# Stores on another queue, a residual chunk per group, inverse steps half a group later

## The chip, the cores and the metric

The kernel runs on one core of one Trainium2 chip. The metric is the device time of one execution in microseconds (us), as the median of repeated runs. Engines are named as in the profile: PE (TensorE), DVE (VectorE), ACT (ScalarE), POOL (GpSimd), SP (SyncE, which here only issues DMAs).

## The reference

Two layers work on x (2 batches, 128 channels, 64 x 64 positions = 4096 tokens). Layer 0 is a block of neighbourhood attention and an MLP. Layer 1 is what the change touches the end of:

```python
t = to_tokens(x)
t = t + attention(layernorm(t))          # 4096 x 4096 scores, per batch
t = t + ffn(layernorm(t))                # spectral filters over the sequence
# ffn, for the chosen branch (of 4): u of shape (b, sl, d)
U_plus  = irfft(rfft(phi)[:, :, None] * rfft(u)[:, None])      # 16 filters, length 8192
U_minus = the same of u with alternating signs, signs put back
out = einsum('btkd,k,kde->bte', U_plus, sigma**0.25, M_plus) + the same with U_minus, M_minus
out = out + sum over 3 lags of shifted u @ M_u[lag]
```

## The kernel before, in words

**Stages.** Layer 0 and the attention of both batches fill the first part (to about 1155 us of the span). A transition (about 1155 to 1197 us) finishes the last token chunks. Then comes the mixing stage, 40 groups of matmuls in about 725 us, and a tail of some 32 us that writes the output.

**The end of the attention.** `after(b, c)` (L1119) is a generator that takes one chunk of 512 tokens from attention to the transform: the softmax quotient and the residual (DVE), a copy into the layout of the scratch tensor `rd` and its store (L1141, L1142), the layernorm (its power is taken by POOL, L174), the transpose (L202), and matmuls with the transform `tr` (L1191, L1205). `store` (L1158) brings the products to DRAM as `us`: ACT copies them from PSUM (L1171), sums and differences are taken (L1176, one half by POOL, one by DVE at the end), and DMAs go out. A chunk has two full stores, of two DMAs of 256 KB each, and a small one, of eight DMAs of 32 KB each (destination 2 x 32 rows of 512 bytes, L1183). `fresh` (L1108) decides who issues: as long as `crowd_[0]` is a list, the DMAs are queued for POOL; once it is None, in the transition, they go out at once on SP (L1110), and the staging tiles `wide` are then cut from the attention's large buffers `e` and `et` (L1163, L1165), two of each. Three small stores (24 DMAs) and five full ones fall into this part. Between these steps PE computes the short lags (L1228), which DVE and ACT bring from PSUM into `xa` (L1249, L1245); PE's and SP's orders are those of the program text, and PE has five PSUM banks for all of these.

**The mixing stage.** A group takes four bins of one batch; a batch has 20 groups (`GROUPS`). For every group:

- four bursts (`burst`, L1588, PE L1597, 16 matmuls each) make the group's y from a block `ct` and an input `ut`, both loaded by SP (four DMAs at L1490, one at L1498). DVE and ACT copy a burst's four PSUM slots (`pc`, four in all) into y (L1602), two each. There are two y tiles, and the bursts of the following group run inside the present one, at k = 0 and 8 of l = 0 and 1.
- 32 projections (`project`, L1612, PE L1616, four matmuls each) add up in four PSUM tiles `acc`, for l in 0..1 and k in 0..15. A burst and eight projections make a quarter of a group.
- `mixed_bins` (L1622) copies `acc` out as `af` (L1626, two by DVE, two by ACT), and POOL folds `af` into the store of bins `ob` in ten operations (L1627 to L1645).

The y tiles of the stage's start lie where the `wide` tiles were: as built, the first copy of y waits for the last small store to have landed.

**The inverse.** When 64 bins of a batch are complete, a generator `back` (L1647) is appended to `rest`, and after a batch's last group `finished` (L1708). A step is taken at k = 4 of each l (L1774): it multiplies what the step before had transposed (L1654; DVE adds the products to `xa`, L1660), and transposes the next two places of `ob` (L1667, ACT copies them, L1668). The first step of `back` only transposes, the last only multiplies. `finished` begins in the same way (L1682) and goes on with products (L1697). A `back` falls behind the 16th group of each batch, `finished` behind the 20th of the first.

**The residual.** `residuals` (L1728) reads `rd` back in 16 chunks: four SP loads (L1734) into one tile `rt`, a 32 x 32 transpose in place by DVE (L1740), an addition to `xa` by POOL (L1742). It is advanced once a burst (L1772); a chunk takes five advances: one for each load, one for the transpose and the addition. DVE's and POOL's orders are made by a scheduler at build time; PE's and SP's are those of the text.

Of the kernel before, what the change touches and what calls it, by code (L numbers as in the profile page):

```python
# [14 lines left out]
P = 128  # L15
# [82 lines left out]
BC = 64  # L98
# [4 lines left out]
def kernel(  # L103
# [16 lines left out]
    nc = tc.nc  # L120
# [14 lines left out]
    for c in range(4):  # L135
# [23 lines left out]
        out=flip, in_=flip, compare_op=ALU.not_equal, fill=1.0, base=1 - QT * QT, pattern=[[0, 2], [1, QT * QT]],  # L159
# [80 lines left out]
    with l0a:  # L240
# [34 lines left out]
        def table(ci, h, eng):  # L275
# [16 lines left out]
            out=gavg, in_=gavg, compare_op=ALU.is_ge, fill=0.0, base=0,  # L292
# [3 lines left out]
            out=gavg, in_=gavg, compare_op=ALU.is_ge, fill=0.0, base=3,  # L296
# [581 lines left out]
    with ap_:  # L878
# [6 lines left out]
        def bank():  # L885
# [6 lines left out]
            out=tr.rearrange("p h e c -> p (h e) c"),  # L892
            in_=nc.inline_tensor(t_in, "t_in").ap().rearrange("(h p) c -> p h c", p=P),
# [208 lines left out]
        def room():  # L1102

            while len({n for _, n, *_ in queued_}) > 3:
                send_one()
            turns_[1] += 1

        def fresh(to, part, by=nc.gpsimd):  # L1108
            if crowd_[0] is None:
                nc.sync.dma_start(out=to, in_=part)  # L1110
                return
            queued_.append((turns_[0], turns_[1], by, to, part))

# [5 lines left out]
        def after(b, c):  # L1119
# [11 lines left out]
            rest = sp.tile([P, 4], F32, tag="rest", name="rest")  # L1131
# [22 lines left out]
            to = zc[b][:, par, s0 : s0 + 2 * P * FB].rearrange("p (c e f) -> p e f c", e=2, f=FB)  # L1154
# [3 lines left out]
            def store(pu, n, r0, m, ri):  # L1158

                if crowd_[0] is None:  # L1160
                    free_[0] = not free_[0]
                    if free_[0]:
                        wide_ = ep.tile([P, 2048], F32, tag="e", name="wide").rearrange("p (a c) -> p a c", c=512)  # L1163
                    else:
                        wide_ = ep.tile([P, 4, 512], F32, tag="et", name="wide", bufs=2)  # L1165
                for s in range(2):
                    if crowd_[0] is None:
                        both, ub = wide_[:, s], wide_[:, 2 + s].rearrange("p (i c) -> p i c", i=2)
                    else:
                        both = sp.tile([P, 512], F32, tag="uo", name="uo", bufs=2)  # L1170
                    nc.scalar.copy(both[:, 0 : 2 * n], pu[s][:, 0 : 2 * n])  # L1171
                    if crowd_[0] is not None:
                        room()
                        ub = sp.tile([P, 2, 256], F32, tag="ub", name="ub", bufs=4)
                    for sgn, op in enumerate((ALU.add, ALU.subtract)):
                        adder[sgn].tensor_tensor(ub[:, sgn, 0:n], both[:, 0:n], both[:, n : 2 * n], op)  # L1176
                    to = us[b, par, r0 : r0 + m, :, :, 2 * hh + s, 2 * fp : 2 * fp + 2]
                    if ri is not None:
                        fresh(to[:, :, ri].rearrange("k g f d -> k g (f d)"), ub)
                        continue  # L1180
                    for sgn in range(2):
                        for f in range(2):
                            fresh(to[:, sgn, :, f].rearrange("k i d -> i k d"), ub[64 * f : 64 * f + 64, sgn, 0:P])  # L1183

            for r0, c0 in row_tiles:
                for ri in range(2):
# [272 lines left out]
        for hh in range(SG // 2):  # L1459
            for e in range(2):  # L1460
# [3 lines left out]
                    out=pns[hh, e].rearrange("p k l f -> p (k l) f"),  # L1464
                    in_=bass.AP(
                        phi_pad.tensor, P - FB + (2 * P * hh + e) * FB, [[2 * FB, P], [PHW, 2 * KF], [1, LG]]
                    ),
# [100 lines left out]
    with ExitStack() as cv:  # L1568
# [8 lines left out]
        def sums(j):  # L1577
            return ps_p.tile([P, 512], F32, tag=f"acc{j}", name="acc")
# [6 lines left out]
        KG = 4  # L1585
        GROUPS = K2 // KG

        def burst(y, kl):  # L1588

            ct, ut = ahead.pop(0)  # L1590
            pcs = [slot() for _ in range(4)]
            for par in range(2):
                cv_ = ct[:, :, 0 : 2 * (FB + 1 + par) * KF].rearrange("p o (l c) -> p o l c", l=2)[:, :, :, 0:TK]
                at = slice(1, 3) if par else slice(0, 4, 3)
                for j in range(4):
                    rows_ = slice(32 * j, 32 * j + 32)
                    nc.tensor.matmul(  # L1597
                        pcs[j].rearrange("p (g o c) -> p o g c", g=4, o=2)[:, :, at], lhsT=ut[rows_, par, :],
                        rhs=cv_[rows_], start=True, stop=True,
                    )  # L1600
            for j in range(4):
                (nc.scalar.copy if j % 2 else nc.vector.tensor_copy)(  # L1602
                    y[:, :, :, 4 * kl + j, :], pcs[j].rearrange("p (g x k) -> p k g x", g=4, k=KF)
                )
            if to_load:
                b_, q_ = to_load.pop(0)
                ahead.append((blocks(q_), inputs(b_, q_)))

        def new_y():
            return cp.tile([P, KF, 4, 4 * KG, 2 * FB], F32, tag="y", name="y", bufs=2)  # L1610

        def project(y, acc, l, k):  # L1612

            for j in range(4):
                rows_ = slice(32 * j, 32 * j + 32)
                nc.tensor.matmul(  # L1616
                    acc[j][:, 0:256], lhsT=(mmi if l else mpl)[rows_, k, :],
                    rhs=y[rows_, k, 2 * l : 2 * l + 2].rearrange("p s n x -> p (s n x)"),
                    start=(l == 0 and k == 0), stop=(l == 1 and k == KF - 1),
                )  # L1620
# [107 lines left out]
        def residuals():  # L1728

            for b in range(NB):  # L1730
                for c in range(NT // 4):
                    rt = cp.tile([P, 4, 4, 32], F32, tag="rt", name="rt", bufs=1)
                    for q in range(4):
                        nc.sync.dma_start(  # L1734
                            out=rt[32 * q : 32 * q + 32].rearrange("p h j i -> p h (j i)"),
                            in_=rd[b, c].rearrange("(h p) q r -> q p h r", h=4)[q],
                        )
                        yield
                    flat = rt.rearrange("p h j i -> p (h j i)")
                    nc.vector.transpose(flat, flat)  # L1740
                    xs = xa[b][:, c * 512 : (c + 1) * 512].rearrange("p (j h r) -> p h j r", j=4, h=4)
                    nc.gpsimd.tensor_tensor(xs, rt, xs, ALU.add)  # L1742
                    yield

        to_add = residuals()
        order_ = [(b, q) for b in range(NB) for q in range(K2)]
        to_load = order_[len(first_blocks) :]
        ahead = list(first_blocks)
        rest = []
        with tc.manual_schedule(engines={mybir.EngineType.PE, mybir.EngineType.SP}):  # L1750
            y = new_y()
            for i in range(4):
                next(lags, None)
                burst(y, i)
            for _ in lags:
                pass
            lags_.close()


            obp = cv.enter_context(tc.tile_pool(name="ob", bufs=1))  # L1760
            ob = obp.tile([P, NB, K2 // BC, 4, 2, BC, 2 * FB], F32, name="ob")
            ob_last = obp.tile([P, NB, 2, 4, LAST, 2 * FB], F32, name="ob_last")
            groups = [(b, g) for b in range(NB) for g in range(GROUPS)]
            for i, (b, g) in enumerate(groups):
                final = i + 1 == len(groups)
                following = None if final else new_y()
                acc = [sums(j) for j in range(4)]
                for l in range(2):
                    for k in range(KF):
                        if following is not None and k % 8 == 0:  # L1770
                            burst(following, 2 * l + k // 8)
                            next(to_add, None)  # L1772
                        project(y, acc, l, k)
                        if rest and k == 4:  # L1774
                            if next(rest[0], None) is None:
                                rest.pop(0)
                mixed_bins(b, g, acc, nc.vector if final else nc.gpsimd)
                y = following
                if (g + 1) * KG % BC == 0:
                    rest.append(back(b, g * KG // BC, [(par, f) for par in range(2) for f in range(FB)]))  # L1780
                if g + 1 == GROUPS and not final:
                    rest.append(finished(b))
            for steps in rest:
                for _ in steps:
                    pass
# [21 lines left out]
        for h in range(2):  # L1807
            o = cp.tile([P, HQ, 2, 2, FB, 2], F32, tag="o", name="o", bufs=2)
            for par in range(2):
                for a in range(4):  # L1810
                    to = place_of(o, par, a)
# [100 lines left out]
```

## Time and profile before

| what | value |
|---|---|
| median of 3 runs | 1960.01 us (1958.05 to 1962.58) |
| the profiled execution: its own time | 1956.34 us |
| its span, first to last instruction | 1954.4 us |
| busy in the span: PE, DVE, ACT, POOL | 1885.4, 960.3, 734.7, 775.9 us |
| PE busy, 1155 to 1197 us (42 us) | 31.63 us, granted clock 0.88 |
| PE busy, 1197 to 1922 us (725 us) | 718.39 us, granted clock 1.00 |
| L1740 DVE transpose of `rt` | 16 times, 711 ns each |
| L1742 POOL addition of `rt` | 16 times, 1271 ns each |

Times in the text are places in the span, in us from its start. A row of the timeline gives the start, the length, the engine, the line, the operation with output and inputs, how many were merged (x) and, in brackets, the idle time of the engine before it and what ended that. Merged matmuls overlap, so the distance between the starts of two bursts tells more than busy time: it is the time of a quarter of a group. "Granted clock" is the share of full speed that PE was given.

### The profile page before, as it was taken

Reading aid. Unit: us, or ns where it says so; the run is one execution under the profiler, and the core shown is the slowest. Engines: PE = TensorE matmul, PEld = TensorE weight load, DVE = VectorE, ACT = ScalarE, POOL = GpSimd, SP = SyncE. Lnnn points to the kernel's source line nnn. Section 1 sums busy time; section 2 is a strip of 40 time slices with the busy share of each in tenths; the row PEclk is TensorE's granted clock in tenths of the full one; section 3 lists DMA queues with packets and bytes.
Section 4 is the critical chain, followed back from the end, with each engine's and each line's share of the span. In section 5 each row is a group of like instructions: output and inputs, shape, how many; then the busy total and the mean of one; then the engine's idle time right before and its main releaser. Section 6 shows DMA issues by size and latency. Waiting matters only on the chain. (4 is left out here: it accounts for less than half of the span.)

```text
span 1954.4 us, 50851 instructions
## 1 busy us (share of the span) xinstructions
PE 1885.4 (96%) x20376; PEld 1343.4 (69%) x20376; DVE 960.3 (49%) x3002; ACT 734.7 (38%) x1742; POOL 775.9 (40%) x1255
## 2 busy tenths in 40 slices
PE   6899998999999999999999998999999999999997
PEld 4677776444444444444444446999998999999986
DVE  5799997454554534454534463333333333333332
ACT  2789887323233323232332242222222222222221
POOL 4366886423743337633443341223332221222211
PEclk8999999999999999999999999999999999999999
DMA  4222221666876545987876422333232223222211
GB/s 155 63 60 59 63 61 41 146 188 215 228 212 190 166 126 164 262 231 227 240 206 180 118 90 74 79 78 79 77 80 60 69 70 90 69 68 67 66 40 45
DMA packets 260394, 234.55 MB, mean 120 GB/s; under 512 B 128095, under 2 KB 214127, under 8 KB 252736
## 3 DMA queue, kind: packets, MB, share of 16 engines
q1 hardware_dynamic: 232290, 133.87, 28.2%
q10 hardware_dynamic: 8126, 58.04, 7.7%
q0 software_dynamic: 19744, 39.39, 6.7%
q8 instruction: 162, 2.65, 0.6%
q14 instruction: 72, 0.59, 0.1%
HBM read 135.59 MB, written 95.45 MB: 118 GB/s over the span
## 5 line engine op out<-in xcount | busy, mean ns | idle before, releaser
L1602 DVE COPY y<-pc 128x512 f32<-128x512 f32 x320 | 205.8, 685 | 326.4 <-PE pc L1597 317.2
L1616 PE MATMUL acc<-y,mpl 32*128 32x256 f32 x5120 | 322.8, 379 | 1.8 <-DVE af L1626 1.7
L1602 ACT COPY y<-pc 128x512 f32<-128x512 f32 x320 | 171.9, 589 | 397.9 <-PE pc L1597 385.0
L1616 PE MATMUL acc<-y,mmi 32*128 32x256 f32 x5120 | 313.7, 375 | 0.0
L1616 PEld LDWEIGHTS acc<-y,mpl 32*128 32x128 f32 x5120 | 291.0, 186 | 10.5 <-DVE af L1626 4.3
L1616 PEld LDWEIGHTS acc<-y,mmi 32*128 32x128 f32 x5120 | 291.2, 185 | 2.8
L1058 PE MATMUL other<-e,tok 128*128 128x512 f32 x448 | 227.3, 593 | 0.0
L932 ACT ACTIVATE e<-bank 128x512 f32<-128x512 f32 x216 | 129.0, 598 | 257.8 <-PE bank L927 253.6
L927 PE MATMUL bank<-cm 128*128 128x512 f32 x432 | 221.8, 600 | 0.0
L1627 POOL TENSOR_TENSOR af<-af 128x512 f32<-128x512 f32 x39 | 49.7, 1275 | 428.4 <-DVE af L1626 415.4
L1597 PE MATMUL pc<-ct,ut 32*128 32x256 f32 x2560 | 210.3, 377 | 6.7 <-ACT y L1602 5.9
L985 PE MATMUL own<-et,tok 128*128 128x512 f32 x448 | 210.3, 593 | 5.0 <-DVE et L975 5.0
L1597 PEld LDWEIGHTS pc<-ct,ut 32*128 32x128 f32 x2560 | 173.3, 186 | 12.0 <-ACT y L1602 6.8
L975 DVE STREAM_TRANSPOSE et<-et 128x512 f32<-128x512 f32 x216 | 134.3, 679 | 87.9 <-DMA et<-eb 87.9
L985 PEld LDWEIGHTS own<-et,tok 128*128 128x128 f32 x448 | 84.6, 190 | 112.7 <-issue 94.2
L1176 POOL TENSOR_TENSOR ub<-uo 128x256 f32<-128x256 f32 (+1 forms) x160 | 99.8, 662 | 148.9 <-ACT uo L1171 136.0
L1058 PEld LDWEIGHTS other<-e,tok 128*128 128x128 f32 x448 | 81.6, 191 | 88.7 <-issue 82.4
L927 PEld LDWEIGHTS bank<-cm 128*128 128x128 f32 x432 | 76.3, 190 | 76.1 <-issue 70.8
L546 ACT ACTIVATE p<-p,mn 128x196 f32<-128x196 f32 x256 | 114.4, 449 | 14.4 <-DVE mn L536 13.8
L1094 POOL DMA_DIRECT2D us<-ub x158 | 107.6, 710 | 9.4 <-DMA us<-ub 7.3
L943 ACT ACTIVATE e<-bank 128x512 f32<-128x512 f32 (+1 forms) x72 | 32.5, 455 | 124.6 <-DVE bank L941 113.3
L536 DVE CUSTOM_DVE_ANT_0 p<-bank,tab 128x196 f32<-128x196 f32 x256 | 76.4, 353 | 4.9 <-PE bank L523 4.7
(274 smaller groups left out, 2639.6 us busy)
## 6 DMA issues: line engine op xcount, KB each, us to landing
eb<-e ACTq DMA_DIRECT2D x54, 1024.0 KB
et<-eb SPq DMA_DIRECT2D x216, 256.0 KB
ut<-us SPq DMA_DIRECT2D x156, 128.0 KB
us<-ub POOLq DMA_DIRECT2D x54, 256.0 KB, 3.6
vw<-vd SPq DMA_DIRECT2D x256, 49.0 KB
ct<-gs SPq DMA_DIRECT2D x312, 40.0 KB
ct<-gs SPq DMA_DIRECT2D x312, 32.0 KB
vd<-v SPq DMA_DIRECT2D x128, 32.0 KB
```

The costliest lines, as they stand in the source:

```text
L536: nc.vector.tensor_tensor_reduce(t[name + "p"][:, h, :], t[name + "S"][h][:, 0:KEYS], tab[:, ci, h, :], 1.0, 3.0e38, ALU.add, ALU.min, t[n ...
L546: nc.scalar.activation(p, p, AF.Exp, bias=t[name + "mn"][:, h : h + 1], scale=-1.0, accum_out=t["den"][:, u, h : h + 1],)
L927: nc.tensor.matmul(ps.rearrange("p (q t j) -> p q t j", q=4, t=4), lhsT=cm[b][:, n * P : (n + 1) * P], rhs=keys.rearrange("p (t q j) -> p ...
L932: nc.scalar.activation(e, ps.rearrange("p (q t j) -> p q t j", q=4, t=4), AF.Exp, bias=0.0, scale=ASCALE)
L975: in_place(nc.vector.transpose(part, part))
L985: nc.tensor.matmul(out_, lhsT=tok[b][:, n, :], rhs=e, start=first, stop=last, skip_group_check=True)
L1058: nc.tensor.matmul(turn(other, "p (q t j) -> p q t j"), lhsT=tok[b][:, n, :], rhs=es[j], start=(j == 0), stop=(j == 3),)
L1094: by.dma_start(out=to, in_=part)
L1176: adder[sgn].tensor_tensor(ub[:, sgn, 0:n], both[:, 0:n], both[:, n : 2 * n], op)
L1597: nc.tensor.matmul(pcs[j].rearrange("p (g o c) -> p o g c", g=4, o=2)[:, :, at], lhsT=ut[rows_, par, :], rhs=cv_[rows_], start=True, stop= ...
L1602: (nc.scalar.copy if j % 2 else nc.vector.tensor_copy)(y[:, :, :, 4 * kl + j, :], pcs[j].rearrange("p (g x k) -> p k g x", g=4, k=KF))
L1616: nc.tensor.matmul(acc[j][:, 0:256], lhsT=(mmi if l else mpl)[rows_, k, :], rhs=y[rows_, k, 2 * l : 2 * l + 2].rearrange("p s n x -> p (s ...
```

## The change

Three edits. (1) The small stores (and only these) are issued by POOL instead of SP once `crowd_[0]` is None. (2) `residuals` issues two loads an advance, and has three stops a chunk instead of five; it is advanced at three of a group's four bursts, not at the first. (3) After a group that completes 64 bins, or the batch, the step of the inverse at l = 0 is left out once; the sequence then begins at k = 4 of l = 1.

```diff
-        def fresh(to, part, by=nc.gpsimd):
+        def fresh(to, part, by=nc.gpsimd, small=False):
             if crowd_[0] is None:
-                nc.sync.dma_start(out=to, in_=part)
+                (nc.gpsimd if small else nc.sync).dma_start(out=to, in_=part)
                 return
...
-                            fresh(to[:, sgn, :, f].rearrange("k i d -> i k d"), ub[64 * f : 64 * f + 64, sgn, 0:P])
+                            fresh(
+                                to[:, sgn, :, f].rearrange("k i d -> i k d"), ub[64 * f : 64 * f + 64, sgn, 0:P],
+                                small=True,
+                            )
...
-                        yield
+                        if q % 2:
+                            yield
+                    yield
                     flat = rt.rearrange("p h j i -> p (h j i)")
                     nc.vector.transpose(flat, flat)
                     xs = xa[b][:, c * 512 : (c + 1) * 512].rearrange("p (j h r) -> p h j r", j=4, h=4)
                     nc.gpsimd.tensor_tensor(xs, rt, xs, ALU.add)
-                    yield
 
         to_add = residuals()
+        fresh_ = [False]
...
                         if following is not None and k % 8 == 0:
                             burst(following, 2 * l + k // 8)
-                            next(to_add, None)
+                            if l or k:
+                                next(to_add, None)
                         project(y, acc, l, k)
-                        if rest and k == 4:
+                        if rest and k == 4 and (l or not fresh_[0]):
                             if next(rest[0], None) is None:
                                 rest.pop(0)
                 mixed_bins(b, g, acc, nc.vector if final else nc.gpsimd)
                 y = following
+                fresh_[0] = (g + 1) * KG % BC == 0 or g + 1 == GROUPS
```

## The prediction

> **What bounds the kernel now.** I read the page first, then busy time by stage, then what PE waits for behind the attention, then the timeline around each of those waits.
>
> ```profile
> PE 1885.4 (96%) x20376; PEld 1343.4 (69%) x20376; DVE 960.3 (49%) x3002; ACT 734.7 (38%) x1742; POOL 775.9 (40%) x1255
> ```
>
> PE bounds the kernel, and in the mixing stage it is never idle for long, so only work taken out of PE's path or a stall counts. PE's waits from 1150 us on are few:
>
> ```profile
> PE pc L1597 <- ACT y L1602: 5.9, 1, 5.9
> ...
> PE pc L1667 <- POOL ob L1640: 2.5, 2, 1.5
> PE pc L1682 <- POOL ob_last L1645: 2.1, 1, 2.1
> PE acc L1616 <- DVE af L1626: 1.7, 3, 0.8
> ```
>
> One is the transition's (edit 1), three are first transposes of an inverse (edit 3), three are group boundaries (edit 2). The waits understate the loss: matmuls slow down after them, so I take the distance between bursts. A plain quarter of a group is 4.32 us (1485.58 to 1489.90); a group's first is 4.40 (1318.87 to 1323.27).
>
> ```profile
> 1475.21 0.41 PE L1597 MATMUL pc<-ct,ut 32*128 32x256 f32 x2
> ...
> 1475.42 0.71 DVE L1740 STREAM_TRANSPOSE rt<-rt 128x512 f32<-128x512 f32 x1 [2.18 <-DMA rt<-rd]
> ...
> 1476.22 1.27 POOL L1742 TENSOR_TENSOR xa<-rt,xa 128x512 f32<-128x512 f32 x1 [12.71 <-DMA ct<-gs]
> ...
> 1477.44 1.27 POOL L1627 TENSOR_TENSOR af<-af 128x512 f32<-128x512 f32 x1
> ...
> 1480.78 2.45 PE L1667 MATMUL pc<-ident,ob 128*128 128x128 f32 x8 [1.52 <-POOL ob L1640]
> ...
> 1485.58 1.03 PE L1597 MATMUL pc<-ct,ut 32*128 32x256 f32 x16
> ...
> 1489.90 1.03 PE L1597 MATMUL pc<-ct,ut 32*128 32x256 f32 x16
> ...
> 1497.36 1.04 PE L1597 MATMUL pc<-ct,ut 32*128 32x256 f32 x16
> ```
>
> In the quarter from 1475.21 PE wants to transpose bins that POOL is still folding; the residual's transpose and addition stand ahead of the folding. It takes 10.37 us. The quarter from 1489.90, with products and transposes in mid-group, takes 7.46 and waits for nobody.
>
> **Edit 3, half a group later.** No work is added. Its price is the transpose step by itself, which the trace shows only with its wait: products and transposes in the third quarter cost 7.46 - 4.32 = 3.15, in a first quarter (1501.67 to 1509.54) 7.87 - 4.40 = 3.47, products alone in a first quarter (1525.65 to 1532.56) 6.91 - 4.40 = 2.51; so transposes alone are about 0.96. POOL ends its folding 6.4 us into the group (1481.84), the moved step is asked for at about 10.8 (two quarters, a burst, 20 matmuls): the wait is gone with 4 us to spare. Steps with products only change places between first and third quarters, two each way: nothing. Then:
> - 1475.21: 10.37 - 4.40 - 0.96 = 5.0 saved
> - 1562.78 to 1570.95 (`finished`): 8.17 - 4.40 - 0.96 = 2.8
> - 1851.27 to 1860.79: 9.52 - 4.40 - 0.96 = 4.2
>
> The last product step of the second batch moves half a group towards the end, into the third quarter of group 19 of 20; a whole group covers it. Bounds: the transposes alone between 0.6 (the eight matmuls and no more) and 1.5; three times that is 1 us either way.
>
> **Edit 2, the residual.** Nothing in the sum of its instructions changes: 64 loads, 16 transposes of 0.71, 16 additions of 1.27. What changes is their place. At three more group starts (1213.35, 1300.18, 1388.10) the transpose stands ahead of DVE's copies of `af`, and PE waits for `acc`: the quarters take 4.73, 5.75 and 4.92, together 2.2 over three times 4.40. In the changed kernel as built, each transpose stands in DVE's queue behind the third burst's copies of y and ahead of the fourth's, one per group in the first 16, and the addition ahead of that group's folding. Saved: 2.2.
>
> The new danger is the transpose's wait. It needs the fourth load, issued on SP behind the third burst's `ut`; behind it in DVE's queue are the fourth burst's copies and the copies of `af`. Before, the last load of a chunk was issued 1.6 to 2.8 us behind its burst's start, and in 16 chunks the transpose began 1.7 to 1.95 (twice 3.1) after that issue's end. A second load in the same advance adds 0.5. So the transpose begins 4.4 to 5.4 us (worst 6.5) behind the third burst; with its 0.71 and two copies (1.29) DVE is free at 6.4 to 7.4 (8.5), and the group ends at 8.63. Cover holds, thinly in the worst case. SP's stretch between bursts is about 0.37 + 2.46 + 2 x 0.47 plus gaps, under 4.32, in two quarters, and less than before in the others; a block is loaded four bursts ahead (17 us), which hides a shift of 1 us. POOL's addition passes ahead of nothing urgent.
>
> **Edit 1, the stores.** This is the part I trust least.
>
> ```profile
> 1158.67 18.80 SPq L1110 DMA_DIRECT2D us<-wide  x24
> ...
> 1181.68 1.07 ACT L1602 COPY y<-pc 128x512 f32<-128x512 f32 x2 [7.52 <-DMA ct<-gs]
> ...
> 1182.32 2.88 PE L1597 MATMUL pc<-ct,ut 32*128 32x256 f32 x16 [5.94 <-ACT y L1602]
> ```
>
> The first copies of y wait for the last small store, issued by SP up to 1177.47; the copy began 4.2 us later. The row blames `ct<-gs`; that load is one of first blocks long in place. With the change SP keeps eight full stores in that stretch and is early, and the last small store is POOL's.
>
> ```profile
> 1070.68 5.88 POOL L1094 DMA_DIRECT2D us<-ub  x9
> us<-ub POOLq DMA_DIRECT2D x16, 32.0 KB, 2.9
> ```
>
> These are the same stores in the attention: 0.65 us each on POOL, landed 2.9 after their start. [...]
>
> Then POOL's queue decides. If the fourth full store's additions start at 1161.43 as before: two additions 1.9, 0.5, four DMAs 2.75, 0.5, four DMAs 2.75, the last chunk's four additions 2.8 to 3.6, and again 0.5 + 2.75 + 0.5 + 2.75: the last issue ends at 1179.1 to 1179.9, landed 2.2 later, 1181.3 to 1182.1, with the copy of y 0.4 behind. That is 0 to 0.8 later than 1181.68: nothing won.
>
> And POOL starts late. The first eight stores (5.4 us) enter its queue between 1142.2 and the layernorm power L174 that DVE and PE wait for:
>
> ```profile
> 1147.63 0.35 DVE L191 TENSOR_SCALAR z<-tt,ln_mv,ln_rs 128x128 f32<-128x128 f32 x1 [1.16 <-POOL ln_rs L174]
> ...
> 1160.93 0.42 PEld L202 LDWEIGHTS bank<-ident,z 128*128 128x128 f32 x4 [0.21 <-ACT xa L1245]
> ```
>
> L174 ended at 1147.59; with 0.56 + 5.5 + 0.56 ahead of the copy (0.61) and itself (1.04) it ends near 1149.9, 2.3 later. DVE runs without a pause from there to 1153.2, so its lag copies (L1249), ACT's behind them (L1245), and PE's banks come 2 us later; PE waits for such a copy already at 1160.93. I carry +2 to 1161.43, of which POOL's contention-free additions give some back: y at 1183.5, **1.8 us later**. Bounds: -0.7 (the 2.3 hidden) to +3.5.
>
> **Sum.** -(5.0 + 2.8 + 4.2) - 2.2 + 1.8 = -12.4. The profiled execution goes from 1956.34 to 1943.9; the runs' median stands 3.7 above that execution, so 1960.0 becomes **1947.6**.
>
> **Rivals.**
> - *The stores cost nothing* (L174's delay is hidden by DVE's and ACT's pauses): -14.2, 1945.8. For it: PE shows no idle time from 1140 to 1160. Against: at 1147.63 DVE waits for L174.
> - *A stall moves*: the step in mid-group meets PSUM slots (`pc`) not yet copied, or POOL costs 3.5: half of the gain, about -6, 1954. Against: mid-group steps with twice the work show no wait.
> - *Slower: the transpose parks DVE.* If `rt` lands late, the fourth burst's copies and `af` slip in every one of 16 groups. Price 1 us for each us that the transpose begins behind 6.6 (8.63 less 0.71 and 1.29); the gain is eaten at 12.4 / 16 = 0.8 more, a start at 7.4. At 8.0, 16 x 1.4 = 22: 1970. Against: landings of 1.7 to 1.95.
> - *The change doesn't do what it says*: DVE's order is the scheduler's; a transpose left at a boundary keeps its loss (2.2 in all): 1949.8, inside the range.
>
> **Chances.** Forecast 0.60, stores free 0.22, stall moves 0.13, slower 0.05. What a measurement can tell from no change is 0.2%, 3.9 us: faster (below 1956.1) has the first two and most of the third, 0.91; same 0.05, slower 0.04. The range 1943.5 to 1953.5 takes the transition's bounds (-2.5, +1.7), 1 us for the transposes, and part of the third case.
>
> **What would show it.** No PE wait on POOL's `ob`; three transposes-only quarters of about 5.3; every group's first quarter 4.40; `rt` transposes 4.4 to 5.4 behind the third burst; the first copy of y near 1183.5 with POOL issuing until 1181. I am wrong if group starts still exceed 4.40, or if the first copy of y is off by more than 2.

## The result and the profile after

| | before | after |
|---|---|---|
| median (runs) | 1958.72 us (6) | 1946.22 us (6) |
| lowest to highest | 1955.23 to 1962.58 | 1942.72 to 1951.01 |
| profiled execution: time, span | 1956.34, 1954.4 us | 1946.17, 1944.5 us |

The ratio is 0.994, with an interval of 0.9922 to 0.9958: 12.5 us less by the medians. In the new listing the lines behind L1110 stand three lower up to the residual (L1597 is now L1600) and five lower there (L1740 is now L1745).

The page's first part has PE with 7 us less busy time, and POOL with 14 us more: 24 DMA issues.

```profile
PE 1878.4 (97%) x20376; PEld 1339.7 (69%) x20376; DVE 959.6 (49%) x3002; ACT 734.4 (38%) x1742; POOL 790.3 (41%) x1279
```

What PE waits for from 1150 us on (total, times, longest):

```profile
PE pc L1600 <- ACT y L1605: 5.7, 1, 5.7
PE acc L1231 <- ACT wide L1171: 3.6, 1, 3.6
PE bank L202 <- ACT xa L1248: 1.4, 1, 1.4
PE pc L1685 <- DVE ob_last L1648: 0.9, 1, 0.9
...
PE acc L1619 <- ACT af L1629: 0.8, 1, 0.8
```

The three waits for POOL's `ob` are gone. The transition's wait for y is still there, and L202 now waits 1.4 us where it waited 0.21. The waits for `wide` (3.7 before) and for `af` are not new: the one for `af`, at 1911.99, is the start of the stage's last group, which waits in the kernel before too (0.76 us at 1922.00).

The inverse's first transposes, in the timeline of POOL and then of PE. The quarter from 1475.21 of before answers to two quarters here, the group's first, now plain, and its third:

```profile
1477.36 1.27 POOL L1630 TENSOR_TENSOR af<-af 128x512 f32<-128x512 f32 x1 [2.48 <-DVE af L1629]
...
1481.51 0.25 POOL L1648 TENSOR_TENSOR ob<-sd 128x32 f32<-128x32 f32 x1
```

```profile
1484.81 0.42 PE L1600 MATMUL pc<-ct,ut 32*128 32x256 f32 x2
...
1485.89 2.52 PE L1619 MATMUL acc<-y,mmi 32*128 32x256 f32 x38
1488.34 1.23 PE L1670 MATMUL pc<-ident,ob 128*128 128x128 f32 x8
1489.50 1.58 PE L1619 MATMUL acc<-y,mmi 32*128 32x256 f32 x24
1490.90 0.39 PE L1600 MATMUL pc<-ct,ut 32*128 32x256 f32 x4
```

The folding ends at 1481.76, the transposes are asked for 6.6 us later and wait for nobody. But their quarter is 1490.90 - 1484.81 = 6.09 us long, where 5.3 was forecast.

The residual's transpose now stands between the copies of y, in DVE's timeline:

```profile
1455.67 0.71 DVE L1745 STREAM_TRANSPOSE rt<-rt 128x512 f32<-128x512 f32 x1 [3.03 <-DMA ct<-gs]
1456.30 1.25 DVE L1605 COPY y<-pc 128x512 f32<-128x512 f32 x2
1459.19 0.76 DVE L1629 COPY af<-acc 128x256 f32<-128x256 f32 x2 [1.64 <-PE acc L1619]
```

DVE then waits for PE (1.64 us at `af`), no longer PE for DVE.

The transition, each engine's rows in order of time, from POOL's last store of the attention on:

```profile
1139.84 1.44 POOL L1094 DMA_DIRECT2D us<-ub  x2
...
1144.14 2.69 POOL L1110 DMA_DIRECT2D us<-wide  x4 [0.30 <-POOL wide L1176]
...
1147.24 2.64 POOL L1110 DMA_DIRECT2D us<-wide  x4
...
1150.46 1.04 POOL L174 TENSOR_TENSOR ln_rs<-ln_rs,mhalf 128x4 f32<-128x4 f32 x1
...
1179.56 2.64 POOL L1110 DMA_DIRECT2D us<-wide  x4
```

```profile
1151.54 0.34 DVE L191 TENSOR_SCALAR z<-tt,ln_mv,ln_rs 128x128 f32<-128x128 f32 x1 [3.40 <-POOL ln_rs L174]
```

```profile
1184.97 1.07 ACT L1605 COPY y<-pc 128x512 f32<-128x512 f32 x2 [7.26 <-DMA us<-wide]
```

The eight issues stand ahead of L174, DVE waits 3.40 us for it (1.16 before), POOL issues until 1182.2, and y begins at 1184.97, where 1181.68 was. Not all of these 3.29 us are the change's. The row at 1139.84 was at 1138.18 in the profile of before, and nothing ahead of it was edited: in ten profiled runs of these kernels it lay anywhere from 1138.18 to 1144.38. So I count from that row's start ("the mark"): the first copy of y comes 45.13 us behind it, before 43.50; 1.63 us later. The mixing stage, counted from its sixth burst (1204.18; before 1200.40) to the end of the span, takes 740.28 us, before 754.04.

### The profile page after: what moved, and what is told of

Read it like the earlier page. It is cut to its first block, busy times and chain, and to the rows that moved or that the text cites. A ratio compares the mean times of both kernels' runs of the same rounds, so it can differ in the third digit from the quotient of the medians.

```text
span 1944.5 us, 50833 instructions
## 1 busy us (share of the span) xinstructions
PE 1878.4 (97%) x20376; PEld 1339.7 (69%) x20376; DVE 959.6 (49%) x3002; ACT 734.4 (38%) x1742; POOL 790.3 (41%) x1279
## 3 DMA queue, kind: packets, MB, share of 16 engines
q8 instruction: 162, 2.65, 0.6%
## 4 chain that ended last, share of the span: by engine, by line
PE 83%; DVE 5%; POOL 4%; DMA 3%; ACT 2%; SPq 1%; issue 1%; ACTq 0%; DVEq 0%; POOLq 0%
PE acc L1619 29%; PE own L985 12%; PE bank L927 9%; PE other L1058 9%; PE pc L1600 7%; PE bank L349 2%; PE bank L936 2%; PE bank L559 2%; PE bank L1194 1%; PE bank L202 1%; DMA et<-eb 1%; PE bank L523 1%; PE pc L1657 1%; ACT p L546 1%; PE po L581 1%
## 5 line engine op out<-in xcount | busy, mean ns | idle before, releaser
L1619 PE MATMUL acc<-y,mpl 32*128 32x256 f32 x5120 | 317.8, 376 | 0.9 <-ACT af L1629 0.8
L1600 PE MATMUL pc<-ct,ut 32*128 32x256 f32 x2560 | 210.4, 377 | 6.4 <-ACT y L1605 5.7
L1600 PEld LDWEIGHTS pc<-ct,ut 32*128 32x128 f32 x2560 | 173.3, 186 | 12.1 <-ACT y L1605 6.5
L1747 POOL TENSOR_TENSOR xa<-rt,xa 128x512 f32<-128x512 f32 x16 | 20.3, 1271 | 170.4 <-DVE rt L1745 170.4
```

Source lines behind the costliest of these rows:

```text
L1600: nc.tensor.matmul(pcs[j].rearrange("p (g o c) -> p o g c", g=4, o=2)[:, :, at], lhsT=ut[rows_, par, :], rhs=cv_[rows_], start=True, stop= ...
L1619: nc.tensor.matmul(acc[j][:, 0:256], lhsT=(mmi if l else mpl)[rows_, k, :], rhs=y[rows_, k, 2 * l : 2 * l + 2].rearrange("p s n x -> p (s ...
```

## The experiments

My theory: edit 3 brings most of the gain, edit 2 a few us, edit 1 costs 1.6 us, because POOL's eight early issues delay L174. The rivals: the residual, not the inverse, was the trouble; the stores are free, or late by their own issuing. Eight kernels were run, four each beside the same runs of before (medians 1957.67 and 1959.27 us). Places come from each kernel's profile: y is the distance from the mark to the first copy of y, mixing the time from the sixth burst to the end of the span. The expectations count y from the end of the marked store, 1.44 less, and one of them counts the stage of the changed kernel from its fifth burst and gives 744.9 (from the start of that burst, 1198.99, it is 745.5).

| kernel | median us | ratio to before (interval) | y | mixing |
|---|---|---|---|---|
| before | 1958.72 | 1 | 43.50 | 754.04 |
| after | 1946.22 | 0.994 (0.9922 to 0.9958) | 45.13 | 740.28 |
| inverse_only | 1948.84 | 0.995 (0.9935 to 0.9966) | 43.61 | 743.39 |
| residual_only | 1953.84 | 0.9983 (0.9973 to 0.9993) | 43.62 | 750.12 |
| stores_only | 1958.43 | 1.0006 (0.9997 to 1.0015) | 45.27 | 752.79 |
| no_stores | 1943.03 | 0.9924 (0.9909 to 0.9939) | 43.65 | 739.89 |
| first_on_sp | 1945.20 | 0.9931 (0.9919 to 0.9943) | 43.26 | 740.14 |
| two_split | 1940.40 | 0.9908 (0.9889 to 0.9926) | 40.32 | 740.29 |
| double_turn | 1950.52 | 0.9956 (0.9943 to 0.9969) | 45.23 | 742.06 |
| late_loads | 1961.24 | 1.0014 (1.0003 to 1.0026) | 45.17 | 757.26 |

### The inverse alone (inverse_only)

The kernel before, with edit 3:

```diff
-                        if rest and k == 4:
+                        if rest and k == 4 and (l or not fresh_[0]):
...
+                fresh_[0] = (g + 1) * KG % BC == 0 or g + 1 == GROUPS
```

> The kernel before with edit 3 alone (the inverse begins half a group later). Theory (edit 3 is most of the gain): 10.5 to 11 us under the kernel before, some 1948; no wait of PE on POOL's ob, the transposes-alone quarters 6.0 to 6.1 us (4.32 and about 1.7), the first quarters still 4.40, and the three long group starts (together 2.2 us over 4.40) still there. Rival (the residual ahead of the folding was what cost the time, and edit 2 carries the gain): 5 us or less.

The mixing stage fell by 10.65 us, from the mark to the end the span fell by 11.1, and the median by 8.8. The transposes-alone quarters have 1.69, 1.68 and 1.69 over 4.32. The two longest of PE's waits from there on:

```profile
PE acc L1616 <- DVE af L1626: 1.8, 2, 0.9
PE pc L1682 <- DVE ob_last L1645: 0.9, 1, 0.9
```

No POOL `ob` is left, and the wait for `af` at group starts still is (it is the residual's). Of the first quarters the long ones had 1.22, 1.47 and 0.13 over 4.32, and a fourth, in the group of the first transposes, 0.49. The theory held: more than three quarters of the gain of the changed kernel's mixing stage come from edit 3.

### The residual alone (residual_only)

The kernel before, with edit 2:

```diff
-                        yield
+                        if q % 2:
+                            yield
+                    yield
...
-                    yield
...
-                            next(to_add, None)
+                            if l or k:
+                                next(to_add, None)
```

> The kernel before with edit 2 alone (residual a chunk a group, turned in mid-group). Theory: the first quarters of the first 16 groups fall from 4.40 to 4.32 and the three long ones with them (2.9 us), and in the quarter that began at 1475.21 POOL's folding no longer stands behind the residual's transpose and addition (1 to 2 us): 4 to 5 us under the kernel before; PE still waits for POOL's ob in two or three places. Rival (edit 2 carries the gain): 8 us or more. Rival (edit 2 does nothing): the first quarters stay 4.40.

The mixing stage fell by 3.92 us and the median by 3.8. The first quarters of the first 16 groups lost 2.8 of it: all but the stage's first are 4.32. The quarter with the first transposes fell from 10.37 to 9.42. A quarter with products near the stage's end lost 0.35, but it lost as much in stores_only, which has no edit 2. The waits that edit 3 removes are still there:

```profile
PE pc L1685 <- POOL ob_last L1648: 2.1, 1, 2.1
PE pc L1670 <- POOL ob L1643: 2.0, 2, 1.0
```

As the theory had it. Edits 2 and 3 together (no_stores, below) give 14.15, the two alone 14.57: they add up to within 0.4.

### The stores alone (stores_only)

The kernel before, with edit 1:

```diff
-                nc.sync.dma_start(out=to, in_=part)
+                (nc.gpsimd if small else nc.sync).dma_start(out=to, in_=part)
```

> The kernel before with edit 1 alone (small stores on POOL). Theory: first copy of y 1.6 us later than before, counted from POOL's last attention store, and the total 1 to 2.5 us up. Rival (stores free): copy and total within 0.5. Rival (the 1.6 of the changed kernel came from the start of the transition and not from the stores): the copy is where it was before.

y came 1.77 us later, and the median was 0.8 higher, with an interval that holds 1; by the span from the mark to the end only 0.4 was lost. The mixing stage, which the edit does not touch, had become 1.25 us shorter. One quarter with a stall gives 1.36 of that, and the other differences nearly cancel. In the profile of before this quarter began at 1475.21, with the transposes at 1480.78 (shown in the prediction) and behind them:

```profile
1483.16 2.58 PE L1616 MATMUL acc<-y,mpl 32*128 32x256 f32 x24
```

Here it begins at 1479.03:

```profile
1484.74 1.98 PE L1670 MATMUL pc<-ident,ob 128*128 128x128 f32 x8 [1.52 <-POOL ob L1643]
1486.64 1.58 PE L1619 MATMUL acc<-y,mpl 32*128 32x256 f32 x24
```

Here is busy time by stretch for the five microseconds behind the stall, in the profile of before and then in this one (bounds, length, busy us of PE, PEld, DVE, ACT and POOL, granted clock, DMA's share and rate):

```profile
1480.70:1485.60 4.90, 4.75 (x36) 3.62 (x40) 0.00 (x0) 1.17 (x2) 1.14 (x6) 0.65 0.03 8
```

```profile
1484.60:1489.00 4.40, 4.20 (x52) 3.51 (x56) 0.00 (x0) 1.07 (x2) 1.19 (x6) 1.00 0.05 10
```

The same stall of 1.52 us, the same 24 matmuls behind it: 2.58 us at a granted clock of 0.65, 1.58 at 1.00. The quarter takes 10.37 us in one and 9.01 in the other. Three finer stretches of before (the clock is the third number from the end) show where the clock was low:

```profile
1480.70:1481.80 1.10, 0.99 (x3) 0.59 (x3) 0.00 (x0) 0.00 (x0) 1.10 (x6) 1.00 0.15 37
1481.90:1485.20 3.30, 3.30 (x25) 2.67 (x29) 0.00 (x0) 1.17 (x2) 0.00 (x0) 0.50 0.00 0
1485.30:1489.00 3.70, 3.70 (x72) 3.35 (x72) 1.29 (x2) 1.07 (x2) 0.00 (x0) 1.00 0.18 52
```

It is one block of half speed, 3.41 us long in the trace (1481.84 to 1485.26). A block of the same length (1857.31 to 1860.72) follows the stall of 1.0 us at 1855.88 of before, and one its like at 1858.36 in stores_only, where it reaches into the next quarter: there the long quarter is 0.57 shorter than in before (9.52), and the one behind it 0.66 longer. So whether a stall of this length also costs clock, and which quarter pays, differs from run to run. And the 2.11 us stall of `finished` (to 1568.39 in before) has no block behind it: the clock is 1.00 from 1568.40 to 1571.40. What opens a block, no run here shows. What this experiment shows of edit 1 is its 1.77 us at y; its median alone does not part edit 1 from nothing.

### Edits 2 and 3 without the stores (no_stores)

```diff
-                (nc.gpsimd if small else nc.sync).dma_start(out=to, in_=part)
+                nc.sync.dma_start(out=to, in_=part)
```

> The changed kernel without edit 1 (small stores on SP as before, edits 2 and 3 in). Theory: the mixing stage as in the changed kernel (744.9 us from its fifth burst to the end), and the first copy of y 1.6 us earlier, counted from POOL's last attention store: 1.6 us under the changed kernel, 14 under the kernel before, some 1944.6. Rival (stores free): equal to the changed kernel within 0.5 in the trace.

y is back at 43.65, 1.5 earlier than in the changed kernel; the mixing stage is within 0.4 of it, and the median is 3.2 under it, though the intervals of the two ratios overlap. So edit 1 takes away a part of what the other two bring; the 1.5 us at y are what is shown of it. Of the 2.8 us that separate the two spans (from the mark), 1.5 lie ahead of y, 1.0 between y and the sixth burst, 0.4 behind. The last two are not shown to be edit 1's (see the stretch behind y in the account of the prediction).

### The first small store back on SP (first_on_sp)

This tells apart why y is late. `small_` counts the small stores in the transition.

```diff
                             fresh(
                                 to[:, sgn, :, f].rearrange("k i d -> i k d"), ub[64 * f : 64 * f + 64, sgn, 0:P],
-                                small=True,
+                                small=small_[0] > 1,
                             )
```

> The changed kernel with the first of the three small stores (8 DMAs) on SP again, the other two on POOL. Theory (POOL's 8 issues ahead of the layernorm power L174 make y late): L174 and the copies behind it 2 us earlier than in the changed kernel, first copy of y 42.0 to 42.9 us behind POOL's last attention store (43.7 in the changed kernel, 42.2 with all on SP), total 1 to 2 us under the changed kernel. Rival (POOL's own row of issues and landings of the last two small stores is what makes y late): L174 early, y still at 43.5 or more.

Rows of POOL, with the mark, and of ACT:

```profile
1144.38 1.44 POOL L1094 DMA_DIRECT2D us<-ub  x2
...
1152.76 1.04 POOL L174 TENSOR_TENSOR ln_rs<-ln_rs,mhalf 128x4 f32<-128x4 f32 x1 [1.06 <-DVE ln_rs L173]
...
1182.19 2.64 POOL L1110 DMA_DIRECT2D us<-wide  x4
```

```profile
1187.64 1.07 ACT L1607 COPY y<-pc 128x512 f32<-128x512 f32 x2 [6.61 <-DMA us<-wide]
```

L174 starts 8.38 us behind the mark (10.62 in the changed kernel), waiting for DVE and not for POOL's issues; y comes at 43.26, that is 1.87 earlier than in the changed kernel and 0.2 to 0.4 earlier than with all stores on SP. The delay was that of the first eight issues ahead of L174. Issuing and landing of the last two small stores on POOL costs nothing against SP. That the last store is what y waits for shows in its landing: here at 1187.49, and the copy of y begins at 1187.64; in the changed kernel 1184.82 and 1184.97. The median is 1.0 under that of the changed kernel, which their spread does not part; the span from the mark is 2.8 shorter.

### Halves on either queue (two_split)

As first_on_sp, and of the last two stores one half each:

```diff
-                                small=small_[0] > 1,
+                                small=small_[0] > 1 and f == 1,
```

> As first_on_sp, and of the last two small stores half of the DMAs on SP, half on POOL. Theory (the last eight DMAs' issuing and landing set the first copy of y, 6 us from either queue alone): y at 39 to 41 us behind POOL's last attention store, total 1 to 3 us under the kernel with edits 2 and 3 alone (1943.0): 1940 to 1942. Rival (the copies before the stores set it): y at 42, total 1943.

Rows of POOL, of ACT and of PE (the mark is at 1141.27):

```profile
1175.83 1.33 POOL L1110 DMA_DIRECT2D us<-wide  x2
```

```profile
1181.59 1.07 ACT L1607 COPY y<-pc 128x512 f32<-128x512 f32 x2 [3.76 <-DMA ut<-us]
```

```profile
1182.45 2.62 PE L1602 MATMUL pc<-ct,ut 32*128 32x256 f32 x16 [2.33 <-DVE y L1607]
```

y comes at 40.32, 4.8 earlier than in the changed kernel and 3.3 earlier than with all on SP. PE's wait falls from 5.68 to 2.33. With 1940.40 us it has the lowest median of the study: 5.8 us under the changed one and 18.9 (0.92%) under before. Its six runs lie between 1936.78 and 1948.00, and its interval overlaps those of no_stores and first_on_sp, so what is shown against these is the gain at y and not the order of the totals. So the last eight small DMAs do set y, from either queue alone.

### The transposes doubled (double_turn)

The changed kernel, in which a chunk's first step writes the same eight transposes twice:

```diff
-                    for a in range(4):
+                    for a in (0, 1, 2, 3) if (par, f) not in places[:2] else (0, 1, 2, 3, 0, 1, 2, 3):
```

> The changed kernel with the first step of each inverse chunk transposing the same two places twice (16 transposes in place of 8, twice in the kernel). Theory (transposes alone cost 1.7 in place of the estimated 0.96 because switching PE between 32-row and 128-row tiles costs some 0.75 at the two ends, and each transpose 0.12): the two quarters grow by 0.9 to 1.0, to 7.0. Rival (each transpose costs 0.21 of PE's path, nothing is fixed): by 1.7, to 7.75. Total within 2 us of the changed kernel plus 1.9 (or 3.4).

```profile
1490.48 2.19 PE L1670 MATMUL pc<-ident,ob 128*128 128x128 f32 x16
1492.60 1.58 PE L1619 MATMUL acc<-y,mmi 32*128 32x256 f32 x24
```

From the first transpose to the next projection it is 2.12 us for 16, and 1.16 for 8: 0.12 each. The two quarters have 2.64 and 2.65 over 4.32, against 1.77 and 1.69 for eight: 0.87 and 0.96 for eight more, and so 0.7 to 0.9 that does not grow. In the rows above the transposes are 128*128 tiles and the projections 32*128 ones; that the change there and back is what the fixed part pays for is my reading: the runs show a fixed cost, and none changes the tile shape alone. The median is 4.3 over the changed kernel, more than the 1.9 expected: the span from the mark is 1.74 longer, and the mark itself lay 2.3 later in the profiled run.

### The second pair of loads issued late (late_loads)

The changed kernel, with the last two of a chunk's four loads issued at the fourth burst of the group, just ahead of the transpose in the program. DVE's order then has the transpose behind the fourth burst's copies of y, ahead of `af`.

```diff
-                        if q % 2:
-                            yield
-                    yield
+                        if q == 1:
+                            yield
+                            yield
...
                     nc.gpsimd.tensor_tensor(xs, rt, xs, ALU.add)
+                    yield
```

> The changed kernel with the second pair of the residual's loads issued one burst later, with the transpose's own advance, so that the transpose waits for its load at the end of the group: the danger that the prediction named, made on purpose. Theory: the transpose begins 5.0 to 5.5 us behind the fourth burst (0.3 to 2.7 in the changed kernel), DVE's copies of af stand behind it, and each of 16 groups is 0.8 to 1.6 us longer: 13 to 25 us over the changed kernel, about 1959 to 1971. Rival (PE does not feel it, the first burst of the next group covers the copies): within 3 us of the changed kernel.

A group in its timeline, DVE and then PE:

```profile
1289.62 0.71 DVE L1745 STREAM_TRANSPOSE rt<-rt 128x512 f32<-128x512 f32 x1 [3.10 <-DMA rt<-rd]
1290.25 0.72 DVE L1629 COPY af<-acc 128x256 f32<-128x256 f32 x2
```

```profile
1290.69 3.84 PE L1619 MATMUL acc<-y,mpl 32*128 32x256 f32 x62 [0.85 <-DVE af L1629]
```

The transposes began 4.5 to 6.0 us behind the fourth burst, that is 0.23 to 1.71 into the next group, and each of the 16 first quarters was 0.54 to 2.03 us over 4.32, together 17.1 us. The quarter grew by about 0.3 more than the transpose was late: 0.23 gave 0.54, 1.71 gave 2.03. The median is 15.0 over the changed kernel, and 0.14% over before. PE feels it us for us, as the slower rival said.

## Why the prediction was right

The total was: 12.4 less forecast, 12.5 less measured. Its terms were right in kind, and some were wrong in size, in ways that cancel. That the two agree to 0.1 us is luck: the interval of the ratio stands for 8.2 to 15.3 us, and in the two profiles the gain from the mark to the end is 11.65 us: 13.76 in mixing, less 1.63 at y and 0.49 behind it.

- **Edit 3: 12.0 forecast, 10.65 measured alone.** The mis-sized term is the "transposes alone", 0.96 us with bounds of 0.6 and 1.5: they cost 1.7 to 1.77, three times 0.75 less gain. The step that failed was the subtraction: a quarter with products and transposes less one with products alone. Both hold the same fixed cost, so the difference is only the 8 x 0.12 of the transposes. Alone, they pay the fixed cost too. That took away 2.2. Against it, the products that change places, put at nothing, gave some 1.1 back: the four of `finished` in first quarters took 5.40 us before and 5.13 in inverse_only; why is open.
- **The margin of edit 3.** The wait for `ob` went, as forecast. The margin was 6.6 us where 4 was forecast, and both of its ends were off. The folding ended 5.6 us into the group (the 1481.84 of before is 6.6 behind 1475.21, not 6.4). The transposes began at 12.2 and not at 10.8: a projection's four matmuls are eight rows of the trace, so 40 rows stand between the burst and the step, not 20.
- **What the stall was worth.** The 10.37 us taken from the one profile held some 1.4 us of lowered clock that the same stall did not cost in another run. The forecast took one draw for the price.
- **Edit 2: 2.2 forecast, 3.92 measured alone.** Forecast were the three long group starts. Not counted were 0.08 at each of these three and at five other starts (0.64), since "every first quarter 4.40" was wrong as a base: in the changed kernel they are 4.32 in the first 16 groups but for the stage's first. Nor was the 0.95 that the residual cost in the quarter of the first transposes; the forecast had put that into edit 3. One reading of the waits was wrong, without harm to the sum, which came from the quarters: of the three waits for `af` only that at 1302.37 (0.83 us) is at a long group start of the residual. The others are 0.15 us at 1902.05 and the last group's 0.76.
- **The transposes' place.** 4.4 to 5.4 us (worst 6.5) behind the third burst was forecast; it was 4.6 to 6.0 in 15 groups, and 7.06 in one. The point from which it costs was put at 6.6. In the changed kernel the one at 7.06 (2.74 behind the fourth burst) cost 0.05, and in two_split one 3.01 behind the fourth cost 0.28. So the point is about 7.0, and the worst case was at the edge of the cover, which late_loads shows to be real.
- **Edit 1: 1.8 forecast, 1.63 measured at y** (1.77 alone), by the mechanism named: L174 late by 2.25 (its start 10.62 behind the mark, before 8.37) against the forecast of 2.3. Without that, "0 to 0.8 later" was forecast for the last stores on POOL, and they came 0.24 earlier. So the row of the trace that the forecast took (0.65 us an issue, 2.9 to landing) was near enough: in the changed kernel the 24 took 0.66 us each and landed 3.1 us after their start (medians). That an issue on SP is shorter (0.53 us in the median of the 34 before) did not decide. POOL's last four full-size additions took 0.72 to 0.74 us each, before 0.90, when DVE was busy beside them: the forecast's "contention-free" was right in size, and no run isolates the cause. What was not forecast is the 0.5 us more from y to the sixth burst (19.21 against 18.72). There the clock was at half speed for 10.2 us from 1182.30, before for 6.8. In the ten kernels this stretch took 17.90 to 19.21, with edit 1 whole 18.39 to 19.21, so the 0.5 is not shown to be the edit's.
- **The rivals.** "The stores cost nothing" is refuted at y by stores_only, no_stores and first_on_sp; "a stall moves" by the changed kernel's waits, none over 0.15 us between the stage's first burst and its last group, though the moved step does pay its fixed cost; "the change doesn't do what it says" by residual_only. The slower one is a real mechanism (15.0 us in late_loads) that the changed kernel just avoids.

## What to carry to other kernels

Put a step that needs a slow engine's result where that result is long ready; a stall costs its wait, and at times nearly as much again in clock (here 1.52 us, and some 1.4 us more in one run of two). Before an issue is moved to another engine's queue, look at which small computation stands behind it: here eight issues ahead of a 1-us operation cost 1.9 us, and what paid was half of the last stores on each queue. To price a step that will stand alone, do not subtract two steps that share a fixed cost.

## What the runs showed of the hardware that was not expected

- The same 1.52 us stall left PE's granted clock at 0.65 over the next 4.9 us in one run and at 1.00 in another. Behind the stalls the clock fell to 0.50 in single blocks of 3.41 us; 1.01 us of stall in residual_only was enough (0.72 over 6 us).
- A step of transposes among the projections costs PE a fixed 0.7 to 0.9 us here, beside 0.12 us for each transpose; that the change of tile (32*128 to 128*128 and back) is the reason is my reading, and no run shows it alone.
- POOL issues a 32 KB store in 0.66 us, and its last one landed 2.6 us after the issue's end; shared by two queues, the last 16 small DMAs let y begin 3.2 to 3.3 us earlier than on SP alone.
- The part of the program ahead of every edit ended at places 6.2 us apart in ten profiled runs, half of the effect studied: stage distances, not places in the span, told the edits apart.
